# Mixing gates in eight tiles of the array, and a new order of the first 620 steps, in a fused convolution, feed-forward and LoRA kernel on one core

## The chip, the core and the metric

The kernel runs on one NeuronCore of a Trainium2 chip. A core has five engines that run side by side, each with its own stream of instructions: TensorE (PE, matrix products; PEld is its loading of the stationary operand), VectorE (DVE), ScalarE (ACT), GpSimd (POOL) and SyncE (SP, which here only issues transfers). Semaphores order them against each other. The metric is the device time of one execution in microseconds (us), as a median of runs; lower is better.

## What is computed

The input x has shape (64, 64, 1024). A grouped 1-D convolution (4 groups, 9 taps) with a conditioning term runs over it; its result, 4096 rows of 1024, goes through a 1024x1024 layer with a shared LoRA and a LoRA that is mixed by gates for each of 8 batches; and x is added at the end.

```python
out = lax.conv_general_dilated(x, weight, ..., padding=[(4, 4)], feature_group_count=4)
out = out + einsum('nd,od->no', c, c_weight)[:, :, None] + bias[None, :, None]
...
base_out = matmul(x, kernel) + bias
A_eff = einsum('bn,nri->bri', gate, lora_A)      # 16 adapters, rank 32, mixed for each of 8 batches
B_eff = einsum('bn,nor->bor', gate, lora_B)
Ax    = einsum('bri,bti->btr', A_eff, x)
delta = einsum('bor,btr->bto', B_eff, Ax)
delta = delta + einsum('or,btr->bto', lora_B_shared, einsum('ri,bti->btr', lora_A_shared, x))
...
return x + base_out + delta
```

The change touches how A_eff and B_eff are made.

## The kernel before

The 64 samples are worked in 16 pairs of tiles ("pairs" 0 to 15), and each pair in four groups g. Two pairs share one batch, so one set of mixed LoRA matrices serves two pairs.

**Precision.** Each operand of the large products is split into a high part and a low part (`hi_of`, `lo_of`), and each product is three matmuls: high by high, high by low, low by high. The splits are most of the work of ACT (the high part), DVE and POOL (the low part: a step ends in `v` for DVE or `p` for POOL).

**One pair.** `xload` fetches the input; the convolution is `xhi`, `xlo`, `conv` for pairs 0 to 2, and for later pairs a form with fewer products (`xdiff`, `xohi`, `xolo`, `xdhi`, `xdlo`, `convo`, `convd`, with `evmid` taking the middle product out of PSUM). `evac` adds the conditioning term, and `turned` transposes on DVE. The dense layer of pair 0 is 8 `plain` steps for each of four blocks (3 matmuls each). From pair 1 on it is 7 products of half-size blocks (`prod`, 12 matmuls each) in place of 8, with sums of blocks made ahead (`asum`, `wsum`) and behind (`xsum`, `ysum`, `radd`, `yadd`). `lora` multiplies by A_eff, and `delta` by B_eff and the bias. `total` adds the input row, and `store` writes. The shared LoRA is folded into the weights once: `fmm` makes a product, `fadd` adds it to the weight tile on DVE.

**The gates.** 16 adapters times 8 rows of a block are laid on the 128 partitions. `lload(w, i)` fetches a piece of lora_A (w=0) or lora_B (w=1), eight pieces each. `gmask` builds a matrix of 128 x 64 that holds the gates on a block diagonal: 8 blocks of 16 adapters. `mix(w, j)`, four for each w, does two matmuls: the stationary operand is that matrix, 128 x 64, the moving operand one piece, 128 x 512. The two write the lower and the upper 64 partitions of one PSUM tile. `mixout` copies that tile to SBUF on ACT, `mixput` writes it to a DRAM buffer `eff[w]` in two transfers, and `aload` and `bload` fetch from there what a batch needs.

**Order.** The text `ORDER` (line 50 on) lists all steps, one after another. Each engine runs its share of them strictly in that order, each queue of transfers too; a semaphore wait holds up everything behind it on the same engine. PSUM is divided by the pools into eight tiles of 128 x 512: two for convolutions (`pcv`), five for all 512-wide sums (`pmm`, tag `mm`: blocks of the dense layer, `fmm`, `mix`), one for `lora`.

Lines that the prediction's steps touch: 318 (`conv`), 364 (`evmid` on ACT), 376 (`evac`), 475 and 479 (`fmm`, `fadd`), 485 (`wsum`), 512 and 513 (`gmask`), 520 (`lload`), 528 (`mix`), 534 (`mixout`), 542 (`mixput`), 550 (`aload`), 556 (`bload`), 580 (`plain`), 592 (`prod`), 602 (`lora`).

Of the kernel before, what the change touches and what calls it, by code (L numbers as in the profile page):

```python
# [10 lines left out]
ALU = mybir.AluOpType  # L11
# [39 lines left out]
small 1, warm, twload 1, busy 29, twload 0, cwload, gload, ctload, cwide, cmul, thi 2, small 0, thi 0, tlo 0 v,  # L51
xload 0 0, xhi 0 0, tlo 2 p, xload 0 1, xlo 0 0 v, conv 0 0, twsum v, xhi 0 1, xlo 0 1 v, conv 0 1, sbload 1,
sbhi 1, csum, evac 0 0 v, turned 0 0, xload 0 2, xhi 0 2, xload 0 3, saload 0, sblo 1 p, xlo 0 2 p, evac 0 1 v,
turned 0 1, saload 1, gmask, xhi 0 3, conv 0 2, xlo 0 3 p, sahi 1, conv 0 3, sahi 0, salo 0 v, fmm 0 1,
sbload 0, sbhi 0, fmm 1 1, wload 1 0, evac 0 2 a, xload 1 0, sblo 0 v, fmm 1 0, salo 1 v, xload 1 1, xhi 1 0,
xhi 1 1, xlo 1 1 p, xlo 1 0 v, turned 0 2, yhi 0 0, ylo 0 0 p, wload 0 1, fadd 0 1, evac 0 3 a, fadd 1 0,
conv 1 0, whi 7 0, fmm 4 0, turned 0 3, xload 1 2, xhi 1 2, wlo 7 0 v, fmm 3 0, wload 1 1, conv 1 1, fadd 1 1,
wload 4 0, fmm 0 0, whi 0 1, wload 0 0, fadd 0 0, evac 1 0 a, plain 0 1 0, fadd 4 0, xlo 1 2 p, turned 1 0,
whi 0 0, wlo 0 1 p, fmm 2 1, fmm 2 0, yhi 0 7, evac 1 1 a, conv 1 2, fmm 5 0, wload 2 1, wload 2 0, fadd 2 0,
wlo 0 0 p, plain 0 0 0, xload 1 3, fadd 2 1, wload 5 0, xhi 1 3, fmm 4 1, xlo 1 3 p, plain 0 0 1, whi 0 2,  # L60
ylo 0 7 v, fadd 5 0, plain 0 3 0, whi 7 1, yhi 0 4, wload 3 0, fadd 3 0, whi 0 3, wload 5 1, fmm 3 1, conv 1 3,
turned 1 1, wlo 7 1 v, wload 3 1, xload 2 0, plain 0 1 1, fadd 3 1, whi 7 2, evac 1 2 v, wlo 7 2 p, wload 4 1,
wlo 0 3 p, wlo 0 2 v, lload 0 6, plain 0 2 0, whi 7 3, plain 0 3 1, fadd 4 1, wload 7 1, turned 1 2, whi 1 1,
plain 0 1 2, lload 0 7, xhi 2 0, plain 0 0 2, ylo 0 4 v, plain 0 3 2, xlo 2 0 v, plain 0 2 1, fmm 5 1,
evac 1 3 a, xload 3 0, wlo 7 3 v, plain 0 2 2, turned 1 3, whi 1 0, yhi 0 1, ylo 0 1 v, fadd 5 1, whi 6 1,
conv 2 0, wload 7 0, thi 1, xdiff 3 0 0 v, wload 6 0, evac 2 0 a, lload 1 5, wlo 1 0 p, fmm 7 0, fadd 7 0,
plain 0 2 3, plain 0 0 3, fmm 6 0, lload 0 2, plain 0 3 3, plain 0 1 3, fadd 6 0, lload 0 5, whi 6 0, asum 1 2,
yhi 1 2, lload 0 0, yhi 1 0, plain 0 0 4, plain 0 2 4, wsum 2 2 v, whi 2 2, lload 1 1, wlo 1 1 p, plain 0 0 5,
fmm 6 1, tlo 1 v, plain 0 2 5, rload 0 2, wlo 6 0 v, wsum 2 1 v, wsum 2 3 v, whi 1 2, wlo 1 2 v, plain 0 1 4,
whi 2 1, asum 1 3, whi 1 3, wlo 1 3 p, xload 2 2, wload 6 1, fadd 6 1, xload 2 1, whi 6 2, lload 0 1, xhi 2 2,  # L70
plain 0 3 4, lload 0 4, plain 0 2 6, lload 1 0, lload 0 3, wsum 2 0 v, fmm 7 1, plain 0 2 7, xload 2 3,
plain 0 0 6, fadd 7 1, whi 6 3, total 0 2, lload 1 6, mix 0 0, mixout 0 0 a, wlo 6 2 v, xhi 2 1, wlo 6 3 v,
wlo 6 1 v, wsum 3 2 v, xlo 2 2 v, mix 0 3, mixout 0 3 a, mix 0 2, mixout 0 2 a, wsum 3 0 v, wsum 5 0 v,
mixput 0 0, whi 2 3, mix 0 1, wsum 3 1 v, mix 1 0, mixput 0 3, mixout 0 1 a, xdiff 3 0 1 p, wsum 4 0 v,
conv 2 2, wlo 2 2 v, whi 2 0, wlo 2 0 v, ylo 1 2 v, plain 0 1 5, wsum 5 1 v, rload 0 0, wsum 5 2 v, wsum 4 2 v,
xlo 2 1 v, plain 0 0 7, mixput 0 1, ylo 1 0 p, mixput 0 2, wlo 2 1 v, prod 1 0, plain 0 1 6, wsum 3 3 v,
wsum 5 3 v, rload 0 1, plain 0 3 5, wsum 4 3 v, bihi, whi 3 2, keep 1 0, plain 0 1 7, lload 1 3, wsum 4 1 v,
plain 0 3 6, mixout 1 0 a, lload 1 7, mix 1 3, aload 0, whi 5 3, yhi 1 3, rload 0 3, lload 1 2, ylo 1 3 v,
mixout 1 3 a, total 0 1, lora 0, mix 1 1, turned 2 0, lora 1, whi 5 0, bilo, xohi 3 0, lload 1 4, mix 1 2,
whi 4 2, wlo 4 2 v, mixout 1 1 a, xolo 3 0 v, whi 3 0, wlo 3 0 v, wlo 3 2 v, yhi 1 1, ylo 1 1 v, mixout 1 2 a,  # L80
asum 1 5, total 0 0, whi 4 1, conv 2 1, axlow 1, axsum 1, xload 3 2, wlo 4 1 p, wlo 2 3 v, whi 4 0,
plain 0 3 7, axlow 0, axsum 0, mixput 1 0, mixput 1 3, wlo 4 0 v, xhi 2 3, xlo 2 3 v, wlo 5 3 v, axhi 1,
prod 1 1, biput 0, axlo 1, whi 3 3, asum 1 6, yhi 1 6, wlo 3 3 v, mixput 1 1, evac 2 1 a, turned 2 1, aload 1,
mixput 1 2, total 0 3, evac 2 2 v, turned 2 2, bload 0 0, whi 3 1, axhi 0, prod 1 2, keep 1 2, conv 2 3,
bhi 0 0, biput 1, yhi 2 0, evac 2 3 a, blo 0 0 v, axlo 0, yhi 1 4, bload 0 1, wlo 3 1 p, prod 1 3, ylo 2 0 v,
delta 0 0 1, total 0 0 1, bhi 0 1, blo 0 1 v, ylo 1 6 p, prod 1 6, whi 4 3, delta 0 3 1, wlo 4 3 v, store 0 0,
ylo 1 4 p, turned 2 3, delta 0 2 1, total 0 3 1, xdhi 3 0, convo 3 0, yhi 1 5, whi 5 1, ylo 1 5 v, xdlo 3 0 v,
delta 1 0, total 0 2 1, xload 3 1, keep 1 3, prod 1 4, evmid 3 0 a, store 0 3, xohi 3 1, xdiff 3 1 0 v,
xdiff 3 1 1 p, wlo 5 1 p, delta 0 1 1, total 0 1 1, wlo 5 0 v, xolo 3 1 p, convd 3 0, evac 3 0, turned 3 0,
asum 2 3, rload 1 0, convo 3 1, yhi 2 1, xdhi 3 1, xdlo 3 1 v, prod 2 0, whi 5 2, store 0 2, delta 1 2,  # L90
xload 3 3, keep 2 0, wlo 5 2 p, yhi 2 3, prod 1 5, total 1 0, xohi 3 3, xolo 3 3 v, asum 2 2, xdiff 3 2 0 p,
store 1 0, convo 3 3, evmid 3 1 a, xdiff 3 2 1 p, convd 3 1, ylo 2 3 v, prod 2 3, rload 1 3, delta 1 1,
ylo 2 1 v, xsum 1, asum 2 5, prod 2 1, xdhi 3 2, evac 3 1, turned 3 1, rload 1 2, radd 1 2 v, xdlo 3 2 v,
xdiff 3 3 0 v, delta 1 3, xohi 3 2, xdiff 3 3 1 p, yhi 2 5, xolo 3 2 v, ylo 2 5 p, yhi 2 2, ylo 2 2 v,
evmid 3 3 a, radd 1 3 v, convo 3 2, total 1 2, store 0 1, evmid 3 2 a, convd 3 2, xdhi 3 3, xdlo 3 3 v,
rload 1 1, radd 1 1 v, bload 1 0, lora 2, axlow 2, asum 2 6, prod 2 2, total 1 1, convd 3 3, evac 3 2,
turned 3 2, axsum 2, xload 4 0, xohi 4 0, xolo 4 0 p, bhi 1 0, yhi 2 4, ylo 2 4 v, axhi 2, prod 2 5, keep 2 3,
yhi 3 0, ysum 1 p, xdiff 4 0 0 v, xdiff 4 0 1 v, prod 2 4, store 1 1, xload 4 1, xohi 4 1, xolo 4 1 p,
yadd 1 v, blo 1 0 v, xdhi 4 0, axlo 2, delta 2 0, yhi 2 6, evac 3 3, keep 2 2, xdlo 4 0 v, convo 4 0,
turned 3 3, convd 4 0, rload 2 0, evmid 4 0 a, total 1 3, total 2 0, ylo 3 0 v, lora 3, xdiff 4 1 0 v,  # L100
xdiff 4 1 1 p, asum 3 3, yhi 3 3, prod 3 0, convo 4 1, ylo 3 3 v, evac 4 0, turned 4 0, xdhi 4 1, xload 4 3,
xohi 4 3, xdlo 4 1 v, asum 3 2, xolo 4 3 v, yhi 3 2, ylo 2 6 v, xload 4 2, xdiff 4 2 0 p, store 1 2,
xdiff 4 2 1 p, xohi 4 2, prod 3 3, yhi 3 1, bload 1 1, evmid 4 1 a, delta 2 2, ylo 3 2 v, xolo 4 2 v, asum 3 5,
store 2 0, convd 4 1, xdhi 4 2, xsum 2, convo 4 2, evmid 4 2 a, evac 4 1, xdlo 4 2 v, rload 2 2, radd 2 2 p,
total 2 2, xdiff 4 3 0 v, xdiff 4 3 1 p, prod 2 6, turned 4 1, yhi 3 4, bhi 1 1, convd 4 2, evac 4 2, keep 3 0,
prod 3 2, ylo 3 1 v, rload 2 3, radd 2 3 v, ysum 2 v, convo 4 3, yadd 2 v, xdhi 4 3, xdlo 4 3 v, ylo 3 4 v,
aload 2, prod 3 1, convd 4 3, turned 4 2, blo 1 1 p, xload 5 0, yhi 3 5, xohi 5 0, keep 3 2, asum 3 6,
keep 3 3, xload 5 1, xohi 5 1, delta 2 3, prod 3 4, delta 2 1, xdiff 5 0 0 p, xdiff 5 0 1 v, axlow 3,
ylo 3 5 p, evmid 4 3 a, total 2 3, prod 3 5, store 2 3, xolo 5 0 p, rload 2 1, yhi 3 6, radd 2 1 p, rload 3 0,
axsum 3, evac 4 3, axhi 3, turned 4 3, yhi 4 0, axlo 3, delta 3 0, xload 5 2, xdhi 5 0, store 1 3, xdlo 5 0 v,  # L110
# [707 lines left out]
```

## Time and profile before

| | |
|---|---|
| median of 3 runs | 447.79 us (447.44 to 451.44) |
| the profiled execution | 447.48 us, of which the span from the first to the last instruction is 445.7 us |
| granted TensorE clock over the span | 1.00 |
| bytes moved | 67.05 MB, mean 150 GB/s |
| mix matmuls (L528) | 32 records, first at 44.1 us, last at 63.3 us |
| lora matmuls (L602) | 512 records, from 59.4 to 420.4 us; the fifth `lora` step starts at 141.04 us |
| transfers of line 520, 256 KB each | 16, 4.6 us from issue to landing in the median |

A matmul of 32-bit operands leaves two records each: 16 mix products are 32 records. The 512-wide matmuls of the dense layer are shown at 391 ns each in a group row, but follow each other every 227 ns: they are pipelined, and it is the distance from start to start that costs time. On DVE a 128x512 instruction is shown at about 0.68 us and the next one starts 0.60 us after it.

### The profile page before, as it was taken

The page shows a single profiled execution, that of the slowest core. Times are in us where ns is not written, and L with a number is a line of the kernel's source. Part 1 is how long each engine was busy: PE and PEld are TensorE (multiplying, and loading weights), DVE is VectorE, ACT ScalarE, POOL GpSimd, SP SyncE. Part 2 cuts the span into 40 slices and gives each one's busy share as a digit, 9 for nine tenths or more (in the row PEclk, how much of TensorE's full clock was granted, in tenths as well). Part 3 has the DMA queues.
Part 4 walks back from the last instruction along what each step waited for, and adds up shares of the span by engine and source line. Part 5 has one row for each costly group of instructions (what it writes and reads, how often), then busy time and mean ns, then how long its engine had stood idle before and what let it go on. Part 6 is the DMA issues. An engine that isn't in the chain of part 4 may idle for free.

```text
span 445.7 us, 7717 instructions
## 1 busy us (share of the span) xinstructions
PE 438.3 (98%) x2557; PEld 358.7 (80%) x2557; DVE 391.3 (88%) x615; ACT 251.2 (56%) x639; POOL 234.5 (53%) x202
## 2 busy tenths in 40 slices
PE   8999999999999999999999999999999999999996
PEld 7677658888888888888878888888888888888884
DVE  5998979899899899889899899899798989887783
ACT  5877468556655566446555655646554745654440
POOL 3766024754747653555444445464656475467543
PEclk9999999999999999999999999999999999999999
DMA  8999582461625463534345453443536354262243
GB/s 229 300 280 308 147 251 66 142 186 49 186 82 158 136 190 110 170 120 136 97 139 147 151 182 91 119 142 90 175 98 186 95 169 151 72 222 90 91 150 118
DMA packets 52488, 67.05 MB, mean 150 GB/s; under 512 B 6112, under 2 KB 34016, under 8 KB 52448
## 3 DMA queue, kind: packets, MB, share of 16 engines
q1 hardware_dynamic: 42512, 49.83, 38.9%
q10 hardware_dynamic: 9936, 16.73, 10.2%
q8 instruction: 20, 0.33, 0.3%
q14 instruction: 20, 0.16, 0.1%
HBM read 47.65 MB, written 18.87 MB: 149 GB/s over the span
## 4 chain that ended last, share of the span: by engine, by line
PE 91%; DMA 4%; DVE 2%; issue 1%; SPq 0%; ACT 0%; ACTq 0%; DVEq 0%
PE mm_a L592 19%; PE mm_d L592 18%; PE mm_c L592 17%; PE mm_b L592 9%; PE cv L346 8%; PE cm L346 4%; PE axp L602 3%; PE cv L318 2%; DMA wr<-in_dram 2%; PE mx L528 2%; PE mm_a L580 1%; PE mm_c L580 1%; DMA ls<-in_dram 1%; DMA ctt<-in_dram 1%; PE mm_d L580 1%; PE mm_a L660 1%
## 5 line engine op out<-in xcount | busy, mean ns | idle before, releaser
L592 PE MATMUL mm_a<-wh,y 128*128 128x512 f32 x240 | 79.6, 392 | 0.0
L592 PE MATMUL mm_d<-wh,y 128*128 128x512 f32 x240 | 79.2, 391 | 0.0
L592 PE MATMUL mm_c<-wh,y 128*128 128x512 f32 x240 | 79.1, 391 | 0.0
L364 ACT ACTIVATE md<-cm,cadd 128x64 f32<-128x64 f32 x208 | 48.2, 315 | 44.8 <-PE cm L346 41.1
L326 POOL TENSOR_TENSOR xf<-xt 128x256 f32<-128x256 f32 x45 | 33.3, 747 | 49.4 <-DVE xd L270 39.4
L265 ACT CAST xd<-xf 128x512 fp32r<-128x512 f32 x52 | 32.5, 626 | 44.9 <-PE cv L346 20.7
L265 ACT CAST y<-s 128x512 fp32r<-128x512 f32 x60 | 37.2, 624 | 30.5 <-POOL s L412 15.3
L592 PEld LDWEIGHTS mm_a<-wh,y 128*128 128x128 f32 x240 | 45.1, 188 | 9.9 <-issue 0.4
L592 PEld LDWEIGHTS mm_d<-wh,y 128*128 128x128 f32 x240 | 45.1, 188 | 9.2 <-issue 0.2
L592 PEld LDWEIGHTS mm_c<-wh,y 128*128 128x128 f32 x240 | 45.1, 188 | 9.1 <-ACT c L636 0.2
L387 DVE STREAM_TRANSPOSE z<-v 128x512 f32<-128x512 f32 x64 | 45.4, 709 | 3.2 <-PE axp L602 1.9
L592 PE MATMUL mm_a<-wl,y 128*128 128x512 f32 x120 | 46.9, 391 | 0.0
L592 PE MATMUL mm_c<-wl,y 128*128 128x512 f32 x120 | 46.8, 390 | 0.0
L592 PE MATMUL mm_d<-wl,y 128*128 128x512 f32 x120 | 46.8, 390 | 0.0
L346 PE MATMUL cv<-xd,th 128*128 128x256 f32 x208 | 45.7, 282 | 0.4 <-DVE xd L270 0.4
L378 DVE TENSOR_TENSOR v<-cv,md 128x512 f32<-128x512 f32 x52 | 35.7, 686 | 7.7 <-PE cv L346 2.5
L270 DVE TENSOR_TENSOR xd<-xf,xd 128x512 fp32r<-128x512 f32 x41 | 34.5, 842 | 7.6 <-ACT xd L265 7.4
L270 DVE TENSOR_TENSOR y<-s,y 128x512 fp32r<-128x512 f32 x49 | 38.2, 782 | 3.0 <-ACT y L265 2.7
L592 PE MATMUL mm_b<-wh,y 128*128 128x512 f32 x120 | 39.6, 391 | 0.0
L346 PEld LDWEIGHTS cv<-xd,th 128*128 128x128 f32 x208 | 35.5, 188 | 2.4 <-DVE xd L270 0.6
L265 ACT CAST y<-z 128x512 fp32r<-128x512 f32 x49 | 30.6, 625 | 11.8 <-DVE c L641 4.5
L326 DVE TENSOR_TENSOR xf<-xt 128x256 f32<-128x256 f32 x59 | 33.7, 587 | 0.2
(132 smaller groups left out, 1008.2 us busy)
## 6 DMA issues: line engine op xcount, KB each, us to landing
xt<-in_dram SPq DMA_DIRECT2D x64, 258.0 KB, 3.2
r<-in_dram SPq DMA_DIRECT2D x64, 256.0 KB, 3.5
out_dram<-r ACTq DMA_DIRECT2D x63, 256.0 KB, 2.6
ls<-in_dram SPq DMA_DIRECT2D x16, 256.0 KB, 4.6
br<-eff SPq DMA_DIRECT2D x48, 64.0 KB, 2.8
wr<-in_dram SPq DMA_DIRECT2D x16, 176.0 KB, 4.2
eff<-ls SPq DMA_DIRECT2D x16, 128.0 KB, 2.7
wr<-in_dram SPq DMA_DIRECT2D x16, 80.0 KB, 3.9
```

The costliest lines, as they stand in the source:

```text
L265: nc.scalar.copy(dst, src)
L270: engs[eng].tensor_tensor(dst, src, f32(hi), ALU.subtract)
L318: nc.tensor.matmul(ps, a[:, 2 * kt, g, :], b[:, :, kt:kt + P], start=(n == 0), stop=(n == 5))
L326: engs[eng].tensor_tensor(xdf[p, g][:, e], m, odd(p, g), ALU.subtract)
L346: nc.tensor.matmul(ps, a[:, w, g, :], b, start=(n == 0), stop=(n == 2))
L364: nc.scalar.activation(t[:, n], cpm[p, g][:, n], ACTF.Identity, bias=c[:, n:n + 1])
L378: nc.vector.tensor_tensor(v.rearrange("p n (i e) -> p e n i", e=2), cps.pop((p, g)), mid.pop((p, g)).unsqueeze(1).to_broadcast([P, 2, 4, H ...
L387: nc.vector.transpose(z[:, :, :, :, gg, :], vs.pop((p, g)).rearrange("p m j -> p (m j)"))
L528: nc.tensor.matmul(mps[w, j][n * e:n * e + n], gm.rearrange("p b i -> p (b i)"), lraw[w, 2 * j + e], start=True, stop=True)
L580: nc.tensor.matmul(acc[p, BLOCKS[b]], m[:, kk, :], n, start=(k == 0 and q == 0), stop=(k == 7 and q == 2))
L592: nc.tensor.matmul(ps, a[:, k, :], b[bb, k], start=s, stop=(k == HK - 1 and q == 2), skip_group_check=not first)
L602: nc.tensor.matmul(axp[q * R:q * R + R, p % 2, :], a[:, k, :], zs[p, hf][:, k, :], start=k < 2, stop=k >= 6)
```

## The change

Two things are changed together.

First, the gates. The stationary matrix is cut in two by partitions: partitions 0 to 63 hold adapters times rows 0 to 3, partitions 64 to 127 rows 4 to 7. Each half is now 64 x 32 instead of being a half of a 128 x 64 matrix with zeros in it. A `mix(w, j)` takes four pieces and does eight matmuls, 64 x 32 stationary and 64 x 512 moving, into two PSUM tiles: four column places times two row halves. There are two `mix` steps for each w instead of four, `mixout` and `mixput` have one more argument, and the layout of `eff` follows. As many copies (8) and transfers (16 of 128 KB for `mixput`) as before.

Second, `ORDER`: the first 624 steps are replaced by 620 others in a new order. From the step `lora 4` on the list is the same, word for word, 1224 steps.

```diff
-    eff = [dram.tile([NC, NB * GC, AW], F32, ...) for w in range(2)]
+    HI = GC // 2
+    eff = [dram.tile([4, NB, 2, 2, 2, HI, AW], F32, ...) for w in range(2)]
-    gm = const.tile([P, NB, GC], F32, name="gm")
+    gm = const.tile([P, NB, HI], F32, name="gm")
...
-        nc.vector.tensor_reduce(mask, ident.rearrange("p (i n) -> p i n", i=GC), AX.X, ALU.add)
+        nc.vector.tensor_reduce(mask, ident.rearrange("p (r i n) -> p i r n", r=2, i=HI), AX.XY, ALU.add)
...
-        mps[w, j] = pl.tile([P, 2 * AW], F32, tag=tag, name=f"mx{w}_{j}")
-        n = NB * GC
-        for e in range(2):
-            nc.tensor.matmul(mps[w, j][n * e:n * e + n], gm.rearrange("p b i -> p (b i)"), lraw[w, 2 * j + e],
-                             start=True, stop=True)
+        for r in range(2):
+            mps[w, j, r] = pl.tile([P, 2 * AW], F32, tag=tag, name=f"mx{w}_{j}_{r}")
+        n, m = NB * HI, P // 2
+        for e in range(4):
+            for r in range(2):
+                nc.tensor.matmul(mps[w, j, r][n * e:n * e + n], gm[m * r:m * r + m].rearrange("p b i -> p (b i)"),
+                                 lraw[w, 2 * e + j][m * r:m * r + m], start=True, stop=True)
...
-    def mixput(w, j):
-        n = NB * GC
-        for e in range(2):
-            dst = eff[w].rearrange("c p a -> p c a")[:, 4 * j + 2 * e:4 * j + 2 * e + 2, :]
-            nc.sync.dma_start(dst, mev[w, j][n * e:n * e + n].rearrange("p (c a) -> p c a", c=2))
+    def mixput(w, j, r):
+        for c in range(2):
+            dst = eff[w][:, :, j, c, r].rearrange("e b i a -> (e b) i a")
+            nc.sync.dma_start(dst, mev[w, j, r][:, c * AW:c * AW + AW])
...
-        nc.sync.dma_start(ar[b].rearrange("p k r -> p (k r)"), eff[0][:, GC * b:GC * b + GC, :])
+        nc.sync.dma_start(ar[b].rearrange("p k r -> p (k r)"), eff[0][:, b].rearrange("e j c r i a -> e (j c r i a)"))
...
-        src = eff[1][:, GC * b:GC * b + GC, :].rearrange("c (e q) a -> c e (q a)", e=2)[:, :, HN * h:HN * h + HN]
+        src = eff[1][:, b].rearrange("e j c r i a -> e (j c r) (i a)")[:, :, HN * h:HN * h + HN]
```

The beginning of the old order and of the new one, and the stretches of the new one around the mixes:

```diff
-small 1, warm, twload 1, busy 29, twload 0, cwload, gload, ctload, cwide, cmul, thi 2, small 0, thi 0, tlo 0 v,
-xload 0 0, xhi 0 0, tlo 2 p, xload 0 1, xlo 0 0 v, conv 0 0, twsum v, xhi 0 1, xlo 0 1 v, conv 0 1, sbload 1,
-sbhi 1, csum, evac 0 0 v, turned 0 0, xload 0 2, xhi 0 2, xload 0 3, saload 0, sblo 1 p, xlo 0 2 p, evac 0 1 v,
-turned 0 1, saload 1, gmask, xhi 0 3, conv 0 2, xlo 0 3 p, sahi 1, conv 0 3, sahi 0, salo 0 v, fmm 0 1,
+saload 0, warm, busy 29, cwload, cwide, small 0, ctload, cmul, sahi 0, twload 1, xload 0 0, twload 0, small 1,
+xload 0 1, thi 2, salo 0 v, gload, thi 0, twsum v, tlo 0 v, xhi 0 0, xhi 0 1, xlo 0 0 v, tlo 2 p, conv 0 0,
+sbload 1, sbhi 1, sbload 0, wload 0 0, xload 0 2, xlo 0 1 v, sblo 1 v, fmm 3 1, xload 0 3, fmm 0 1, fmm 1 1,
+sbhi 0, gmask, sblo 0 v, fmm 0 0, csum, xhi 0 2, fadd 0 0, whi 0 0, evac 0 0 v, turned 0 0, conv 0 1,
+evac 0 1 v, bihi, wload 0 1, fadd 0 1, wload 1 0, turned 0 1, xlo 0 2 p, xhi 0 3, fmm 2 0, wlo 0 0 p, conv 0 2,
+xload 1 0, xhi 1 0, wload 2 0, wsum 2 0 v, xlo 0 3 p, conv 0 3, yhi 0 0, xlo 1 0 v, saload 1, whi 7 0,
+evac 0 2 v, wlo 7 0 p, turned 0 2, sahi 1, salo 1 v, thi 1, xload 1 1, xhi 1 1, xlo 1 1 p, fmm 1 0, conv 1 0,
...
+whi 3 0, wsum 5 1 p, plain 0 3 1, plain 0 2 7, rload 0 0, total 0 2, wsum 2 2 v, plain 0 0 5, plain 0 1 4,
+mix 0 1, plain 0 0 6, xlo 2 0 v, whi 6 3, plain 0 3 2, lload 1 0, mixout 0 1 0 a, lload 0 6, mixout 0 1 1 a,
+mix 0 0, wlo 6 3 v, lload 1 6, mixout 0 0 0 a, xload 2 1, whi 2 2, plain 0 3 3, plain 0 0 7, xhi 2 1,
...
+prod 1 0, plain 0 3 4, lload 1 4, asum 1 3, mixput 0 0 0, mixput 0 1 0, mixput 0 1 1, wsum 3 3 v, whi 2 3,
+wlo 2 2 v, wsum 4 1 v, xlo 2 1 v, wlo 2 0 v, whi 6 2, wlo 6 2 v, mixout 0 0 1 a, mixput 0 0 1, total 0 0,
+yhi 1 3, wsum 5 3 v, mix 1 0, plain 0 3 5, mixout 1 0 0 a, xload 2 2, plain 0 1 6, conv 2 1, wsum 5 2 v, bilo,
+lload 1 7, lload 1 5, wsum 4 2 v, whi 3 1, wsum 4 3 v, wlo 2 3 p, plain 0 1 7, evac 2 0 a, wlo 3 1 v, xhi 2 2,
+wlo 3 2 v, mixout 1 0 1 a, whi 2 1, asum 1 2, wsum 4 0 v, whi 5 3, plain 0 3 6, xload 3 0, wlo 3 0 v, mix 1 1,
+aload 0, lora 0, ylo 1 3 v, whi 3 3, xlo 2 2 v, xdiff 3 0 0 v, xdiff 3 0 1 v, mixout 1 1 0 a, mixout 1 1 1 a,
```

In the replaced stretch some steps also go to another engine. Net, DVE has 197 instructions there instead of 192, ACT 199 instead of 219 (five `evmid` steps of pairs 3 to 5 go from ACT, four instructions each, to DVE, one each), POOL 67 as before, SP 123 as before, PE 674 instead of 658. Everything else that is computed is the same.

## The prediction

> **What bounds the kernel now.** I read the page first: busy time by engine, and the chain that ended last.
>
> ```profile
> PE 438.3 (98%) x2557; PEld 358.7 (80%) x2557; DVE 391.3 (88%) x615; ACT 251.2 (56%) x639; POOL 234.5 (53%) x202
> ...
> PE 91%; DMA 4%; DVE 2%; issue 1%; SPq 0%; ACT 0%; ACTq 0%; DVEq 0%
> ```
>
> TensorE is the bound, VectorE is next to it. A busy PE need not be a full one, so I checked the distances: 45 matmuls start from 25 to 35 us, one per 0.222 us, against 0.227 us between 512-wide matmuls of the dense layer. So PE has no holes there, and what is to shorten the span must take work from PE, or remove holes at the start. The second view is busy time in stretches (columns: stretch, its length, then busy us and instructions of PE, PEld, DVE, ACT, POOL, then clock, DMA share, GB/s). 138.6 us is where DVE starts the first instruction of the part of the list that is not changed.
>
> ```profile
> 0.00:12.00 12.00, 10.17 (x53) 8.96 (x54) 7.20 (x11) 5.65 (x9) 4.75 (x10) 1.00 0.85 229
> 12.00:138.60 126.60, 125.51 (x680) 96.66 (x679) 116.33 (x180) 81.82 (x198) 67.15 (x56) 1.00 0.61 182
> 138.60:214.00 75.40, 75.40 (x460) 63.21 (x459) 67.94 (x110) 43.69 (x113) 41.74 (x36) 1.00 0.47 141
> 214.00:234.00 20.00, 19.57 (x127) 16.16 (x126) 18.98 (x30) 11.41 (x34) 8.15 (x9) 1.00 0.37 117
> ```
>
> DVE is busy for 92% of the changed stretch after 12 us, 90% up to 214 us and 95% up to 234 us, where PE has to wait for it once (0.43 us). ACT and POOL have room. The third view is the timeline of PE around the mixes: the rows tell from start to start what a mix costs.
>
> ```profile
> 44.10 4.74 PE L528 MATMUL mx<-ls,gm 128*64 128x512 f32 x20
> 48.77 0.50 PE L318 MATMUL cv<-xsh,th 128*128 128x512 f32 x1
> ...
> 57.19 2.24 PE L528 MATMUL mx<-ls,gm 128*64 128x512 f32 x4
> 59.36 1.08 PE L602 MATMUL axp<-z,ar 128*32 128x128 f32 x32
> 60.80 1.08 PE L528 MATMUL mx<-ls,gm 128*64 128x512 f32 x4 [0.35 <-DMA ls<-in_dram]
> 61.81 1.08 PE L602 MATMUL axp<-z,ar 128*32 128x128 f32 x32
> 62.82 1.08 PE L528 MATMUL mx<-ls,gm 128*64 128x512 f32 x4
> 63.83 0.50 PE L318 MATMUL cv<-xs,th 128*128 128x512 f32 x1
> ```
>
> The last view is the first microseconds of PE, DVE and ACT, where transfers and splits set the pace.
>
> ```profile
> 7.47 0.48 PE L318 MATMUL cv<-xsh,th 128*128 128x512 f32 x1
> 11.62 0.51 PE L318 MATMUL cv<-xsl,th 128*128 128x512 f32 x1 [0.62 <-POOL xsl L270]
> 16.35 0.50 PE L318 MATMUL cv<-xsl,th 128*128 128x512 f32 x1 [0.37 <-DVE xsl L270]
> 4.78 1.50 DVE L727 COPY cwe<-cwt 128x512 f32<-128x512 f32 x1 [3.65 <-DMA cwt<-in_dram]
> 12.43 0.99 DVE L513 TENSOR_TENSOR gm<-gg,mask 128x64 f32<-128x64 f32 x1
> 8.15 0.62 ACT L265 CAST sb<-sbr 96x512 fp32r<-96x512 f32 x1 [1.23 <-DMA sbr<-in_dram]
> ```
>
> **The mixes.** Removed: eight mixes of two products, four records each. From start to start: 4.67 us for five (44.10 to 48.77), 2.17 for one (57.19 to 59.36, with waits for a piece and for `aload 0`), 1.01 for each of the last two, and 0.35 us of waiting ahead of one: 9.2 us, of which about 1.6 are waits. Added: four mixes of eight products. Inside a mix of before the two products run side by side: its four records start in two pairs, 0.43 us apart, so a mix is two rounds of 0.43 us and 0.15 us for entering and leaving, 1.01 us alone. `lora` does the same with four products of 32 columns: its 32 records start in eight groups of four, 0.11 us apart. If all eight tiles of a new mix run at once, it is again two rounds, 1.01 us, and some 7 ns for each further start: 1.07 us, 4.3 us for four. What no row of this trace shows is two row halves at once. The ends: at once, 4.3 us; in turn, four rounds, 1.87 us each, 7.5 us. The Trainium skill, "TensorE: Matmul & The Clock Gate", section "Part 3: Packing small matmuls", measured 6.32 times for nine tiles and 10.6 for sixteen, so about 5.6 for eight (an estimate from its table): eight products alone, 8 x 0.86 = 6.8 us, by 5.6 are 1.22 us, with 0.15 for entering 1.37 us, 5.5 us for four. The rows of the trace give two and four columns at nearly their full factor, so I take their side: 4.3 us, a gain of 9.2 - 4.3 = 4.9 us with the waits gone. By the skill's figure it is 3.7 us, in turn 1.7 us.
>
> A rule that speaks against the change: the Trainium skill, "TensorEngine Tiling (Array Packing)", section "Gotcha 1: PSUM Pressure", says that row tiles write to different PSUM banks, and so need more of them. Here a mix takes two of the five tiles `mm` at once. Three blocks of pair 0 hold the other three, so `mix 0 0` must wait for both copies of `mix 0 1`. In the list two `plain` steps (6 matmuls, 1.36 us) stand between; two copies of 0.59 us (line 534) need 1.2 us. Hidden, just; without that cover up to 1.2 us. I charge nothing.
>
> **The start.** Here the new list does more ahead of the first convolutions. By the trace, DVE instructions follow each other at 0.60 us, and transfers land at the pace of before (bytes in order of issue). `saload 0` (192 KB) and `xload 0 0` now stand ahead of `twload 0`, so both halves of the convolution's weights are in at about 7.2 us, not before 4.6 us. Then on DVE: `twsum`, `tlo 0`, `xlo 0 0` end at 9.0 us; the third matmul of the first convolution starts at about 9.1 us and the sixth ends its turn at 10.0 us (before: 8.95). Behind it stand four `fmm`, ahead of the second convolution. The first waits for `sblo 1` (10.2 us). The fourth waits for `sblo 0`, which stands on DVE behind mask and gates (0.3 + 0.8, the 0.99 row with half the columns): 12 us. The second convolution, queued behind it, starts at 12.2 us; before it started at 8.96. From there `conv 0 2` follows at 13.9, `conv 0 3` waits for POOL (`xlo 0 3` behind `wlo 0 0`, 1.3 us each) to 16.6, `conv 1 0` for `evac 0 2` on DVE, which frees its PSUM tile at 18.0, `conv 1 1` for `evac 0 3` on ACT (20.0), `conv 1 2` for `evac 1 0` (22.2). The first `plain` step ends at 24.4 us. Work done by then: 42 matmuls of line 318 at 0.236, 9 of line 475 at 0.235, 3 of line 580 at 0.227, together 12.7 us: 11.7 us behind the clock. Before, at 25 us: 42, 10 and 11 matmuls, 14.8 us: 10.3 behind. So 1.4 us are lost at the start, 1.5 taken; the ends are 0 (transfers land earlier) and 3 us. From 24 us on I find the splits ahead of the `plain` steps by 0.5 us and more.
>
> **VectorE.** DVE gets five instructions more (0.69 us, line 376 or 378, 0.60 from start to start), and with the other exchanges about 2.6 us. Before, it was busy for 123.5 of 138.6 us; the 15 us of idle time are 4.5 at the start, about 5 released by PE, about 3 by ACT. Now: 123.5 + 2.6 = 126.1 busy, 5.3 at the start, 3 to 5 by ACT: 134.4 to 136.4 us. PE, 3.4 us earlier (4.9 - 1.5), wants it at 135.2 us. So the gain can just pass, at 97% busy from 12 us on; I charge 0.6 us. If the cover is gone, see the second rival. Past `lora 4` nothing is changed; DVE has 7.5 idle us up to 214 us, more than half of it released by PE, which shrink when PE is early.
>
> **Queues.** ACT loses 20 instructions (5 x 0.93 us), nothing is late for it. POOL: same count. SP: same transfers in another order; the two pieces `lload 1 7` and `lload 1 5` stand behind `mixput 0 0 1`, which waits for `mixout 0 0 1` on ACT, and `mix 1 1` needs them. I find that copy near 50 us, the pieces landing (4.2 us and two issues) near 56 us and PE there at 57: hidden, by a microsecond; before, such waits were the 1.6 us at 57 to 61 us. They could come back as 0 to 2 us; I charge 0.4. `aload`, `bload`, `biput`, `store`: same sizes and counts, covered as before by what PE does meanwhile.
>
> **Sum**, on the profiled execution of 447.48 us: -4.9 + 1.5 + 0.6 + 0.4 = -2.4, 445.1 us. The median stands 0.31 above that execution, so 445.4 us.
>
> **Rivals.**
> First, all of it lands: no loss at the start, no wait on DVE: 447.8 - 4.9 = 442.9, and 442.4 if the wait of 0.43 us at 233 us goes too. For it: PE's holes of before at the start (0.62 and 0.37 us) show that waits there are short. Against it: the walk above.
> Second, slower: VectorE becomes the bound of the changed stretch. If it stays only as dense as before, 92% after 12 us, its 126.1 - 7.2 = 118.9 us need 129.4 us, with 0.8 us more at the start 142.2 us in place of 138.6: 3.6 us later, 451.4 us; the unchanged part can give some back from its idle time. It decides from 94.5% on: above that the change gains. For it: 95% from 214 to 234 us is the densest such stretch of the unchanged part, and only with PE waiting. Against: about a third of its idle time was PE's doing.
> Third, the rows take their turn, or PE's gain is eaten by waits for pieces: -1.7 + 1.5 + 0.6 + 0.4 = +0.8, 448.6 us.
>
> **How the numbers follow.** A measurement of this kernel can tell about 1%, 4.5 us. The forecast (443.5 to 447) 0.47, all lands 0.15 (nearly all of it over 1%), third rival (447 to 449.5) 0.16, slower (449.5 to 454 and beyond) 0.22, of which 0.15 are over 1%. Faster by over 1% (below 443.3): 0.14; within: 0.71. The range for 8 in 10 reaches from 442.4 to 451.8; the forecast's own is 443.5 to 447.
>
> **What would show it.** Four mixes of 16 records in about 1.07 us each (eight starts within 0.1 us, then again after 0.43 us): the gain; 1.9 us: rows in turn. The second convolution starting near 12 us, and the first `plain` step near 24 us. `lora 4` on PE near 138 us in place of 141.04. DVE's busy share from 12 us on 95% or more, and DVE among the releasers of PE between 70 and 234 us. It would be wrong if PE shows several waits for DVE, or for `ls`, of over a microsecond after 40 us.

## The result, and the profile after

The changed kernel takes 453.3 us in the median of nine runs (451.3 to 455.4), the kernel before 447.8 us: a ratio of 1.010 (95% interval 1.007 to 1.013). It is slower by 1%, and outside the range of the prediction. The profiled execution took 453.34 us, its span is 451.6 us. Two slow executions among the experiments, one of 615 us (`after_w512_again`, the profiled one, so that it has no distances below) and one of 2,470 us (`before_y160`), are left out of all figures.

The page's first and fourth part of the changed kernel:

```profile
PE 441.2 (98%) x2589; PEld 357.2 (79%) x2589; DVE 394.4 (87%) x620; ACT 246.5 (55%) x619; POOL 236.6 (52%) x202
...
PE 79%; DMA 8%; DVE 7%; issue 3%; SPq 2%; ACT 1%; POOL 1%; DVEq 0%; ACTq 0%; POOLq 0%
```

TensorE was to save 4.9 us on the mixes and their waits, and is busy 2.9 us longer than before. Busy time by stretches (columns as in the prediction: stretch, length, PE, PEld, DVE, ACT, POOL, clock, DMA share, GB/s):

```profile
0.00:12.00 12.00, 9.48 (x46) 8.14 (x46) 5.39 (x11) 5.68 (x9) 2.24 (x8) 1.00 0.79 216
12.00:138.60 126.60, 123.66 (x715) 95.56 (x715) 116.17 (x185) 76.26 (x177) 70.45 (x56) 1.00 0.59 183
138.60:214.00 75.40, 75.27 (x453) 61.86 (x452) 68.66 (x108) 43.23 (x112) 41.52 (x35) 1.00 0.44 137
214.00:234.00 20.00, 20.00 (x129) 16.59 (x128) 17.41 (x28) 10.90 (x31) 9.29 (x9) 1.00 0.37 118
```

From 138.6 to 234 us, where (but for the first 3 us) the list of steps is the same word for word, PE is idle for 0.13 of 95.4 us, at full clock, and yet does 582 matmuls where it did 587 before. DVE is busy for 91% and 87% of the two stretches (before 90% and 95%). So no engine holds PE up there: PE itself does its work more slowly. (The chain in the fourth part leaves PE more often than before, 79% against 91%, but in this stretch without idle time of PE.) The mixes are not the reason; PE's timeline around them:

```profile
42.75 1.09 PE L532 MATMUL mx<-ls,gm 64*32 64x512 f32 x16
...
45.37 1.09 PE L532 MATMUL mx<-ls,gm 64*32 64x512 f32 x16
...
53.59 1.09 PE L532 MATMUL mx<-ls,gm 64*32 64x512 f32 x16
...
59.01 1.42 PE L532 MATMUL mx<-ls,gm 64*32 64x512 f32 x16
62.02 1.19 PE L605 MATMUL axp<-z,ar 128*32 128x128 f32 x36 [1.59 <-DMA ar<-eff]
```

Three mixes take 1.02 us from start to start, the fourth 0.33 longer, and then the first `lora` waits 1.59 us for its piece of A_eff. The cost is in the dense layer. The group rows of its products (busy us in all, mean ns of one), first of the kernel before, then of the changed one:

```profile
L592 PE MATMUL mm_a<-wh,y 128*128 128x512 f32 x240 | 79.6, 392 | 0.0
L592 PE MATMUL mm_d<-wh,y 128*128 128x512 f32 x240 | 79.2, 391 | 0.0
```

```profile
L595 PE MATMUL mm_a<-wh,y 128*128 128x512 f32 x240 | 80.6, 396 | 0.0
L595 PE MATMUL mm_d<-wh,y 128*128 128x512 f32 x240 | 80.4, 396 | 0.0
```

Each is about 5 ns longer, with no idle time ahead of it. The timeline shows the same from start to start, before and after, near 301 us:

```profile
301.12 0.40 PE L592 MATMUL mm_d<-wh,y 128*128 128x512 f32 x1
301.35 0.39 PE L592 MATMUL mm_d<-wl,y 128*128 128x512 f32 x1
301.58 0.62 PE L592 MATMUL mm_d<-wh,y 128*128 128x512 f32 x2
302.03 0.39 PE L592 MATMUL mm_d<-wl,y 128*128 128x512 f32 x1
302.26 0.62 PE L592 MATMUL mm_d<-wh,y 128*128 128x512 f32 x2
```

```profile
300.12 0.62 PE L595 MATMUL mm_c<-wh,y 128*128 128x512 f32 x2
300.58 0.40 PE L595 MATMUL mm_c<-wl,y 128*128 128x512 f32 x1
300.82 0.62 PE L595 MATMUL mm_c<-wh,y 128*128 128x512 f32 x2
301.28 0.40 PE L595 MATMUL mm_c<-wl,y 128*128 128x512 f32 x1
301.52 0.62 PE L595 MATMUL mm_c<-wh,y 128*128 128x512 f32 x2
```

Before, five starts take 1.14 us, 228 ns each; after, six take 1.40 us, 233 ns. Over the whole trace the mean is 228.4 ns before and 233.5 ns after (distances within one line of the dense layer, those over 260 ns left out). There are 1,356 such products, and as many records: their operands are cast to fp32r (line 265), and each leaves one record; it is the products of plain float32, the mixes and `lora`, that leave two. 1,356 x 5.1 ns = 6.9 us. The other matmuls keep their distances (the half-size convolution 117 to 118 ns, line 318 at 236 ns in both), so it is not the clock. A span 5.9 us longer is thus 6.9 us lost in the dense products and about 1 us gained elsewhere.

### The profile page after: what moved, and what is told of

It is laid out like the page before. It is cut to its first block, busy times and chain, and to the rows that moved or that the text cites. A ratio compares the mean times of both kernels' runs of the same rounds, so it can differ in the third digit from the quotient of the medians.

```text
span 451.6 us, 7752 instructions
## 1 busy us (share of the span) xinstructions
PE 441.2 (98%) x2589; PEld 357.2 (79%) x2589; DVE 394.4 (87%) x620; ACT 246.5 (55%) x619; POOL 236.6 (52%) x202
## 4 chain that ended last, share of the span: by engine, by line
PE 79%; DMA 8%; DVE 7%; issue 3%; SPq 2%; ACT 1%; POOL 1%; DVEq 0%; ACTq 0%; POOLq 0%
PE mm_a L595 16%; PE mm_d L595 15%; PE mm_c L595 15%; PE mm_b L595 8%; PE cv L346 7%; PE cm L346 4%; PE axp L605 3%; DMA xt<-in_dram 2%; PE cv L318 2%; DMA ar<-eff 1%; DMA gg<-in_dram 1%; PE mm_a L583 1%; PE mm_c L583 1%; DMA r<-in_dram 1%; DMA out_dram<-r 1%
## 5 line engine op out<-in xcount | busy, mean ns | idle before, releaser
L595 PE MATMUL mm_a<-wh,y 128*128 128x512 f32 x240 | 80.6, 396 | 0.0
L595 PE MATMUL mm_d<-wh,y 128*128 128x512 f32 x240 | 80.4, 396 | 0.0
L595 PE MATMUL mm_c<-wh,y 128*128 128x512 f32 x240 | 80.4, 396 | 0.0
L364 ACT ACTIVATE md<-cm,cadd 128x64 f32<-128x64 f32 x188 | 43.7, 316 | 37.5 <-PE cm L346 33.3
L270 DVE TENSOR_TENSOR y<-s,y 128x512 fp32r<-128x512 f32 x48 | 37.1, 775 | 4.4 <-ACT y L265 4.1
L270 DVE TENSOR_TENSOR xd<-xf,xd 128x512 fp32r<-128x512 f32 x41 | 32.7, 798 | 4.7 <-ACT xd L265 4.3
L270 POOL TENSOR_TENSOR xd<-xf,xd 128x512 fp32r<-128x512 f32 x11 | 15.2, 1384 | 34.1 <-ACT xd L265 34.1
```

The source lines that it names most:

```text
L270: engs[eng].tensor_tensor(dst, src, f32(hi), ALU.subtract)
L364: nc.scalar.activation(t[:, n], cpm[p, g][:, n], ACTF.Identity, bias=c[:, n:n + 1])
L595: nc.tensor.matmul(ps, a[:, k, :], b[bb, k], start=s, stop=(k == HK - 1 and q == 2), skip_group_check=not first)
```

## The experiments

**What could make one kind of product slower.** Where the tiles lie in SBUF is read from the compiled kernels. A pool gives its tags their places in the order of first use, so a new order of steps moves them. The dense products read a weight tile (moving operand, tag `w`: `wh`, `wl`) and a tile `y` (stationary). Their start addresses modulo 512 are 320 and 320 in the kernel before, 32 and 192 in the changed one. My first theory was that a weight tile that starts 32 past a multiple of 64 is read more slowly; the rival, that the pace comes with the new order in some other way. Four kernels, each with small unused tiles put ahead of others:

```diff
 after_w64:   -saload 0, warm, busy 29, ...
              +pad 8 gapa, saload 0, warm, pad 8 gapb, busy 29, ...      (two tiles of 8 floats around tag w)
 before_w32:  -conv 0 1, sbload 1, sbhi 1, ...
              +conv 0 1, pad 8 gapa, sbload 1, pad 8 gapb, sbhi 1, ...
 after_all64: +    const.tile([P, 8], F32, name="gap")
              and the slots of xsh, xsl, xs rounded up to a multiple of 64 bytes
 after_w512:  after_all64 with  +pad 112 gapa, saload 0, ...
+    def pad(n, name):
+        work.tile([P, n], F32, tag=name, name=name, bufs=1)
```

> The changed kernel, with 32 bytes of unused SBUF before the tiles of the weights (the moving operand of all dense products) and 32 after them: the weight tiles start at a multiple of 64 bytes again, as in the kernel before, and by pads nothing else changes its place by other than 64 bytes. Theory (place of the weight tiles): the dense products' distance from start to start falls from 232 ns to 227 ns, 1,350 of them by 5 ns are 6.7 us, and the time falls from 453.3 to about 446.6 us. Rival (the chip or the run was slower, or the mixes leave TensorE slower): 232 ns stays, about 453 us. Rival (VectorE is the bound): 232 ns or less, and the time stays within 1.5 us of 453.

> The kernel before, with 32 unused bytes before the weight tiles and 32 after them, so that they start 32 bytes past a multiple of 64. Nothing else is changed. Theory (place of the weight tiles): the distance rises from 227 to 232 ns, and the time from 447.8 to about 454 us. Rivals: 227 ns and 447.8 us stay.

> The changed kernel with every operand of TensorE but the inputs of the first three pairs' convolutions at a multiple of 64 bytes (a pad behind the gates, and longer slots for the split inputs). If the place of any moving operand counts, the 256-wide convolution products (118 ns, 468 of them) and the 64 products with the bias row (236 ns) get faster as well, by 2 to 9 ns each: 1.5 to 3 us below the run that moves the weight tiles alone, some 444 us. If only the weight tiles count: as that run. If places don't count: 453 us.

> As the run before, with the weight tiles at a multiple of 512 bytes instead of 64. If a coarser grid than 64 bytes counts, the distance falls below 227 ns, down to 213 ns at the least (two rounds of the mix took 0.427 us for 512 columns), that is up to 19 us less. If 64 bytes is the grid, 227 ns and the same time as the run before within 1 us.

In kind, all four went as the first theory said: 228.6 to 229.8 ns for the three with `w` at a multiple of 64, 233.0 ns and a ratio of 1.011 for the kernel before with `w` moved by 32. (All numbers are in the table below.) In time, `after_w64` came down to 449.2 us only, where 446.6 was written, and neither the further gain of other operands (some 444 us) nor that of a coarser grid came. The loss is the place of the tiles, then, not the order's waits. Two more kernels go with them: `before_all64`, the kernel before with the same rounding of the slots,

> The kernel before with every operand of TensorE but the inputs of the first three convolutions at a multiple of 64 bytes; its weight tiles were there already. If the weight tiles are nearly all of the effect: 447.8 us within 1 us. If the other operands count too: up to 2 us less, and the ranking of the two kernels at equal places changes by as much.

which changed nothing in time (1.0004), so rounding by itself brings no gain; and `after_w512` once more, on another chip,

> The kernel with the weight tiles at multiples of 512 bytes once more, as the base of the three others on this chip. If its first result was no accident of a chip, its ratio to the kernel before is 0.997 again (0.995 to 0.999), with a mean of 228.6 ns from start to start of the dense products.

which gave 0.998 (0.996 to 0.999).

**The first theory falls.** Here only `y` is moved, in `after_w512`, with the weight tiles left at multiples of 512 (the tags behind `y` move by 64 bytes in the first, by 256 in the second):

```diff
 w512_y32:  -xload 1 0, ...
            +pad 8 gapy, xload 1 0, pad 8 gapz, ...      (xload 1 0 makes the first tile of tag y)
 w512_y64:  +pad 16 gapy, xload 1 0, pad 48 gapz, ...
```

> The base, with the other operand of the dense products (the stationary one, the tiles `y`) moved by 32 bytes, from 256 to 288 in 512; the weight tiles stay at multiples of 512. Theory (the place of the moving operand alone counts): mean distance of the dense products 228.5 to 230 ns, time as the base within 2 us. Rival (either operand at 32 past a multiple of 64 costs 5 ns): 233 ns, and 6 to 7 us more than the base.

> The base, with the stationary operand `y` moved by 64 bytes, from 256 to 320 in 512, the weight tiles as in the base. If the small second effect is one of the distance between the two operands (a difference of 64 in 256 costs, none at a multiple of 256): the difference is now 192 in 256, so the mean distance is over 229.3 ns if any non-zero difference counts, and 228.6 ns if only 64 does or if the effect has another cause. Time within 2 us of the base either way.

Both lost the gain, at 232.9 and 233.2 ns. The first alone could be read as "either operand at 32 past a multiple of 64"; the second, with both operands at multiples of 64, cannot, and it lost 3.6 us against its base where I had written within 2. The difference of the two places, modulo 256, which I had taken for a small second effect, fits all runs so far. As it was seen only behind these results, four more kernels tested it: the changed kernel with only `y` moved, so that the difference is 0 again while the weight tiles stay at 32 past a multiple of 64; the kernel before with the difference of the changed one; and two differences not seen until then.

```diff
 after_y96:    +pad 24 gapy, xload 1 0, pad 40 gapz, ...
 before_y160:  +pad 40 gapy, xload 1 0, pad 24 gapz, ...
 w512_y128:    +pad 32 gapy, xload 1 0, pad 32 gapz, ...
 w512_y224:    +pad 56 gapy, xload 1 0, pad 8 gapz, ...
```

> The changed kernel, with one thing moved: the tiles `y` (stationary operand of the dense products) by 96 bytes, from 192 to 288 in 512. The weight tiles, the moving operand, stay at 32 past a multiple of 64; the difference of the two is then a multiple of 256 as in the kernel before. Theory (the pace follows the difference of the two operands' places, modulo 256): mean distance of the dense products 228.3 to 229 ns in place of 233.5, span 446 to 448 us, time 447 to 449 us. Rival (a moving operand at 32 past a multiple of 64 costs 5 ns each): it stays at 233 ns, and at 453 us.

> The kernel before, with the tiles `y` moved by 160 bytes, from 320 to 480 in 512; the weight tiles stay at a multiple of 64 (320 in 512). The difference is then what it is in the changed kernel (96 in 256). Theory of the difference: 233.5 ns in the mean in place of 228.4, some 6.5 us longer: 454 to 455.5 us. Rival (place of the moving operand alone): as the kernel before.

> The version with weight tiles at multiples of 512, with `y` moved by 128 bytes, to 384 in 512: a difference of 128 in 256, not seen so far. Theory of the difference: it lies on a curve with 228.6 ns at 0, 229.8 at 64, 233.5 at 96, 233.2 at 192 and 232.9 at 224; I expect 231 to 235 ns, and 450 to 454 us. Rival (place of the moving operand alone): 228.6 ns, and 447.7 us.

> The same with `y` moved by 224 bytes, to 480 in 512: a difference of 32 in 256, not seen so far. Theory of the difference: between 228.6 and 233.5 ns, over 229.3; 448.5 to 454 us. Rival (place of the moving operand alone): 228.6 ns, and 447.7 us.

Each time is a ratio to the kernel before, measured beside it; each distance is the mean of one profiled execution, and `w512_y224` was run twice only.

| kernel | w, y (mod 512) | w - y (mod 256) | mean ns, start to start | time against the kernel before (95%) |
|---|---|---|---|---|
| before | 320, 320 | 0 | 228.4 | 1 |
| before_all64 | 448, 448 | 0 | 228.8 | 1.000 (0.999 to 1.002) |
| after_all64 | 64, 320 | 0 | 228.9 | 0.999 (0.998 to 1.001) |
| after_w512 | 0, 256 | 0 | 228.6 | 0.997 (0.995 to 0.999) |
| after_y96 | 32, 288 | 0 | 228.5 | 0.996 (0.995 to 0.998) |
| w512_y224 | 0, 480 | 32 | 233.2 | 1.007 (1.004 to 1.010) |
| after_w64 | 64, 256 | 64 | 229.8 | 1.001 (0.999 to 1.003) |
| after | 32, 192 | 96 | 233.5 | 1.010 (1.007 to 1.013) |
| before_y160 | 320, 480 | 96 | 233.6 | 1.010 (1.007 to 1.013) |
| w512_y128 | 0, 384 | 128 | 232.7 | 1.007 (1.006 to 1.009) |
| w512_y64 | 0, 320 | 192 | 233.2 | 1.006 (1.005 to 1.008) |
| w512_y32 | 0, 288 | 224 | 232.9 | 1.007 (1.004 to 1.009) |
| before_w32 | 352, 384 | 224 | 233.0 | 1.011 (1.007 to 1.015) |

Kernels with one difference agree whatever their order and their absolute places: 96 in two orders (233.5, 233.6), 224 in two (232.9, 233.0), 0 in five places. A difference of 0 in 512 (before) and one of 256 in 512 (`after_w512`) are alike, so it is 256 that counts. No place of one operand alone does it: `w` at 0 and `y` at 320 stand in quick rows, and together in a slow one. The group rows of `after_y96`, and then of `before_y160`, have changed sides against the rows above:

```profile
L596 PE MATMUL mm_a<-wh,y 128*128 128x512 f32 x240 | 79.4, 392 | 0.0
L596 PE MATMUL mm_d<-wh,y 128*128 128x512 f32 x240 | 79.1, 391 | 0.0
```

```profile
L592 PE MATMUL mm_a<-wh,y 128*128 128x512 f32 x240 | 80.8, 397 | 0.0
L592 PE MATMUL mm_d<-wh,y 128*128 128x512 f32 x240 | 80.5, 396 | 0.0
```

So 96 bytes ahead of the tag `y` take the loss out of the changed kernel (a ratio of 0.996 in place of 1.010) and bring its own gain to light, and 160 bytes put the same loss into the kernel before (454.7 against 448.9 us on that chip). The smaller gate tile lies ahead of both tags and moves both by the same 128 bytes, so it is the order of first use that changed the difference. Why the difference of two addresses sets the pace was not tried.

**The gates without the new order.** The old order, with the four new mixes in the places of old ones, and the tiles where they lie in the kernel before:

```diff
-mix 0 0, ... mix 0 3, ... mix 0 2, ... mix 0 1, ... mix 1 0, ... mix 1 3, ... mix 1 1, ... mix 1 2
+mix 0 0, ...              mix 0 1, ...                            mix 1 1, ...              mix 1 0
```

> The old order of steps, with the four new mixes put where eight old ones stood, and the tiles where they are in the kernel before. If the mixes' TensorE time is what they are worth in place: the first group of five old mixes (4.7 us) becomes two new ones of 1.02 us with a wait of 1.2 us for the two copies between them, and the other three (4.5 us with waits) become two: 3 to 4 us less than before, 444.5 us. If what follows was waiting for something else anyway (the split of the next convolution's input on VectorE, the LoRA matrices from DRAM): less than 1.5 us, 446.5 to 448 us.

A miss: 452.5 us on a chip where the kernel before takes 449.0, a ratio of 1.008 (1.006 to 1.010), at a mean distance of 228.3 ns. The eight-tile mixes alone do not make the kernel faster. PE's list of waits (us in total, times, longest):

```profile
PE dl L664 <- DVE axt L627: 2.4, 1, 2.4
PE mx L533 <- DVE r L670: 1.2, 1, 1.2
...
PE mx L533 <- ACT ls L539: 0.7, 1, 0.7
```

The last line is the cost that the prediction named and charged nothing for: a mix takes two of the five `mm` tiles at once, and `mix 0 1` waits for the copy of a tile of `mix 0 0`. The old order has no two `plain` steps there to cover it. The second line is the same shortage once more: the second half of a mix waits until a `total` on DVE gives a tile back. The first line, a `delta` of pair 0 waiting for the LoRA sums, costs more than its 2.4 us. The stretches ahead of it, the wait, and behind it:

```profile
62.00:75.60 13.60, 13.11 (x70) 9.51 (x67) 12.11 (x19) 10.41 (x25) 5.74 (x4) 1.00 0.32 101
75.60:78.20 2.60, 0.41 (x2) 0.00 (x0) 1.98 (x4) 1.63 (x5) 0.00 (x0) 1.00 0.32 87
78.20:82.20 4.00, 3.75 (x10) 3.01 (x11) 3.20 (x6) 3.48 (x9) 1.28 (x1) 0.60 0.37 131
```

In the 4 us behind the wait the granted clock is 0.60 in the mean (0.50 from 79.0 to 82.4 us), and PE starts 10 matmuls where it starts 17 or 18 at full clock: 4.0 x 0.4 = 1.6 us more. The waits and the clock are 5.9 us (2.4 + 1.2 + 0.7 + 1.6), of which 1.2 stood in the expectation: 4.7 of the some 7 us between a gain of 3.3 and a loss of 3.5. The rest was not traced.

**The wait ahead of the first `lora`.** In the changed kernel `aload 0` is issued at 55.4 us and its data lands at 62. Two ways to take the 1.4 to 1.6 us back, both from `after_w512`, and one that also changes the start:

```diff
 after_ar:         -mix 1 1, aload 0, lora 0, ...
                   +... mixput 0 0 1, aload 0, ...  mix 1 1, lora 0, ...
 after_ar_start:   after_ar, with twload 1, twload 0, small 1, xload 0 0, xload 0 1 ahead of saload 0
 w512_conv_ahead:  -mix 1 1, aload 0, lora 0, ylo 1 3 v, whi 3 3, xlo 2 2 v, ... conv 2 2, ...
                   +mix 1 1, aload 0, ylo 1 3 v, whi 3 3, xlo 2 2 v, conv 2 2, lora 0, ...
```

> The changed kernel with the weight tiles at 512 bytes, and the load of the first mixed lora_A ahead of three other loads in SyncE's queue. In the changed kernel the first lora step waits 1.6 us for that load. Expected: the load is issued 2 to 3 us earlier and the wait goes, some 1.5 us less than the same kernel with the load where it was (447.7 us), 446.2 us; but if VectorE holds TensorE back soon after, the wait comes back as another one before 100 us and the time is within 0.5 us of 447.7.

A miss: 449.3 us, a ratio of 1.001 (1.000 to 1.002) where `after_w512` has 0.997. The wait went from `lora 0` to `mix 1 1`. In SP's queue (start, length of the issues) `aload 0` now stands ahead of the last two pieces:

```profile
46.32 6.28 SPq L548 DMA_DIRECT2D eff<-ls  x8
54.38 0.65 SPq L556 DMA_DIRECT2D ar<-eff  x1
55.09 0.42 SPq L293 DMA_DIRECT2D xt<-in_dram  x1
55.56 0.98 SPq L525 DMA_DIRECT2D ls<-in_dram  x2
```

In `after_w512` the pieces are issued at 52.5 us, here at 55.6, since the queue stands 1.8 us (52.60 to 54.38) at `aload 0`; `mix 1 1` waits 1.62 us (the list of waits puts it down to ACT, the queue to its pieces). And again the clock falls: the stretches of that wait and behind it,

```profile
57.00:60.60 3.60, 2.05 (x7) 0.69 (x5) 1.72 (x4) 1.08 (x3) 0.00 (x0) 1.00 1.03 301
60.60:64.60 4.00, 3.92 (x58) 2.32 (x62) 1.97 (x5) 3.68 (x9) 0.43 (x1) 0.57 0.98 334
```

> As the run before, and the start as it was in the kernel before in one respect: both halves of the convolution's weights are loaded first, then the inputs, then the shared LoRA. Expected: the first convolution starts near 7.6 us instead of 8.9, and 1 to 1.5 us of the 1.9 lost at the start come back: some 445 us. If VectorE is the bound of the stretch up to 140 us, it gives less than 0.5 us.

A miss too: 452.1 us, 1.008 (1.006 to 1.010). The first convolution starts 0.5 us earlier than in `after_w512` (7.17 us), but an `fmm` then waits 2.5 us for its operand, the clock is 0.56 for the 3.8 us behind, and the second convolution starts at 13.4 us in place of 11.6. The rearranged first uses have also moved the tiles, to a difference of 64: 229.9 ns.

> The base, with the steps `ylo 1 3 v`, `whi 3 3`, `xlo 2 2 v` and `conv 2 2` moved ahead of `lora 0`, so that TensorE has six convolution products to do while the piece of A_eff for `lora 0` is still on its way. Theory (the wait of 1.4 us ahead of `lora 0` is a hole on the path that sets the end, and its cover was taken away by the gain of the mixes): the wait goes, `lora 4` starts 1.2 to 1.4 us earlier than in the base, near 137.6 us, and the span is 1 to 1.4 us shorter, near 443.9 us; time near 446.4 us. Rival (VectorE is as dense as TensorE there and takes the gain back): the wait for the piece goes, but waits for VectorE appear behind it, and `lora 4` starts within 0.5 us of the base. A second rival: the later `lora 0` makes a wait at the first `delta` as in the old order with the new mixes.

The wait for the piece is gone, as intended, and nothing is gained: 448.05 us, 0.997 (0.995 to 0.999), beside 448.2 us of its base on the same chip, and `lora 4` at 138.99 us where the base, profiled on another chip, has 138.92. The list of waits of PE from 55 us on begins with:

```profile
PE cv L348 <- ACT v L376: 1.0, 1, 1.0
PE cv L348 <- DVE xd L270: 0.4, 1, 0.4
PE mm_c L598 <- DVE y L270: 0.4, 1, 0.4
PE cm L348 <- ACT md L366: 0.3, 1, 0.3
```

Its rival said this in kind: PE runs into the next late producer. The largest wait is for ACT, at 74.3 us, not for VectorE.

## Why the prediction was wrong

**The step that failed** is a term of the sum that was put at nothing: "Past `lora 4` nothing is changed". The sum took every dense product at the 227 ns of the kernel before and asked only what the change does to other work. The new order moves the tiles, since a pool places a tag at its first use, and each dense product then takes 5.1 ns longer. The term left out is +6.9 us; with it the sum is -2.4 + 6.9 = +4.5, 452.0 us for the profiled execution, which took 453.34.

**The mixes: right.** Forecast 1.07 us each, measured 1.02 where nothing is waited for: the eight tiles, two row halves among them, run at once. The estimate from the table of the Trainium skill, "TensorE: Matmul & The Clock Gate", "Part 3: Packing small matmuls" (1.37 us), and "rows in turn" (1.87 us) are out. The wait of `mix 0 0` for its PSUM tiles was hidden, as written: it starts 0.33 us behind the last `plain` matmul, like the first mix.

**The start: right within its ends.** The second convolution starts at 12.88 us (forecast 12.2); the first `plain` step starts at 24.88 and ends its turn at 25.58 (forecast 24.4 for the end). Summing what each PE start in the first 40 us is late against the usual distance of its shape gives 4.6 us, against 2.2 before: 2.4 us in place of 1.5. It scatters: over three variants of each order that share the first steps (before, `before_w32`, `before_y160`; after, `after_y96`, `after_w512`) it is 2.2 to 3.4 and 3.2 to 4.6 us, 1.4 between the means.

**Waits for pieces: too small.** Charged 0.4 us; measured 0.33 inside the last mix and 1.59 at `lora 0`, 1.9 us. (At `lora 0` it scatters: 0.3 to 1.9 us in the nine kernels with the new order.) The text looked at the pieces `ls` and set `aload` aside as "covered as before by what PE does meanwhile". But nothing is left for PE to do meanwhile: all mixes are done at 60.43 us, where the kernel before had two of them behind `lora 0`. SP's queue, the first line of the kernel before, then the changed one:

```profile
54.82 0.56 SPq L550 DMA_DIRECT2D ar<-eff  x1
```

```profile
47.23 5.79 SPq L545 DMA_DIRECT2D eff<-ls  x8
53.07 0.58 SPq L293 DMA_DIRECT2D xt<-in_dram  x1
53.75 0.95 SPq L522 DMA_DIRECT2D ls<-in_dram  x2
54.76 0.46 SPq L293 DMA_DIRECT2D xt<-in_dram  x1
55.39 0.66 SPq L553 DMA_DIRECT2D ar<-eff  x1
```

Before, `lora 0` starts at 59.36 us, 4.5 us behind the issue of `aload 0`. Here the load stands behind eight transfers and four loads, is issued 0.6 us later, and takes 6.6 us to land. Why it takes 2 us longer is open: the DMA engines are as full (a share of 1.00 from 55.4 to 62 us, 0.98 from 54.8 to 59.4 us before).

**`lora 4`: right at equal pace.** It starts at 141.81 us, forecast near 138. It has 360 of the dense products ahead of it, 1.8 us of the loss; without that, 140.0. Taken over all variants, each with its own pace put back to 228.4 ns (the excess of its mean distance times 360 ahead of `lora 4`, times 996 behind it, is subtracted), `lora 4` starts at 141.0 to 142.5 us in four kernels with the old order (old mixes) and at 137.6 to 140.0 in nine with the new order and the changes above to the tiles' places alone: a gain of 3.1 us between the means. The forecast was 3.0 (141.04 to 138; PE's timeline has 140.97 for the first), the sum 2.4.

**VectorE: charged 0.6 us, not seen.** PE waits for DVE for 0.9 us from 12 to 138.6 us, all of it before 20 us and so part of the start. At equal pace too DVE stays under the 95% that the text named as a sign: in `after_y96` it is busy for 116.1 of 124.6 us (12 to 136.6), 93%.

**Behind `lora 4`: a second miss, hidden by the first.** The text let the gain of the head pass to the end. With the pace put back in the same way, the rest takes 304.1 to 305.1 us in the four kernels with the old order and 304.7 to 305.0 in the five new ones with a slow pace, but 305.9 to 306.9 in the four with a pace of 228.5 to 229.8 ns. So the unchanged part gives back 1 to 2 us of the gain when PE is both early and quick. In part it shows among the waits of PE after 138 us; in `after_y96`:

```profile
PE cv L347 <- DVE xd L271: 0.4, 1, 0.4
PE cm L347 <- ACT md L365: 0.3, 1, 0.3
PE cv L347 <- DVE v L379: 0.3, 1, 0.3
PE mm_c L596 <- DVE y L271: 0.2, 1, 0.2
```

The kernel before has only the first of these, and so has `after_w512`, where the rest takes 305.9 us. The waits too short for this list were not traced further, so the cause of this miss stays open in the main.

**The rivals.** The second gave 451.4 us, near the result by luck, by a mechanism that did not happen: VectorE is busy for 91.8% of 12 to 138.6 us, and after 20 us PE does not wait for it. The third (448.6 us) is right in one half: waits for pieces do eat gain, but the rows do not take turns. The first (442.9 us) would have needed no waits at all; the best version run, `after_y96`, is at 0.996 (0.995 to 0.998) of the kernel before, 448.0 against 448.9 us on its chip. So with the tiles in place the change gains 0.9 of the 2.4 us of the sum.

## What to carry to other kernels

A new order of steps, or a tile of another size between two others, moves where tiles lie against each other: before a changed order is judged, compare the mean start-to-start distance of the commonest matmul in both traces, and put the two operands back to the same distance in SBUF if it differs. A forecast that moves first uses should carry this as a term, here 5 ns by 1,356 products. A wait that is taken away is worth only what the next late producer lets through, and a wait of a few microseconds on TensorE can cost 1.7 to 2 times its length where the clock falls behind it (three waits here), and its own length where it doesn't.

## What the runs showed of the hardware that was not expected

- The pace of a 512-column matmul of fp32r operands, stationary 128 x 128, depends on the difference of the operands' addresses in SBUF modulo 256 bytes: 228.3 to 228.9 ns at 0, 229.8 to 229.9 at 64, 232.7 to 233.6 at 32, 96, 128, 192 and 224 (160 was not run). The absolute places, multiples of 64 or not, make no difference beyond 0.6 ns.
- Eight tiles of 64 x 32 (four column places, two row halves) work at once on float32 operands: 1.02 us for eight products of 512 columns, as long as two of 128 x 64 before.
- Behind three waits on TensorE the granted clock was 0.50 for 3.4 us, beginning 0.2 to 0.5 us after the wait's end: 2.44 us (`old_order_new_mix`, 79.0 to 82.4 us), 2.48 us (`after_ar_start`, 11.7 to 15.1) and 1.62 us (`after_ar`, 61.2 to 64.6). After 1.59 us in the changed kernel and 1.90 us in `after_all64` it stayed at 1.00, so the length alone does not tell. The Trainium skill, "TensorE: Matmul & The Clock Gate", "Part 1: The HAM clock gate", has half the clock after an idle window of about 3.4 us that runs freely; the half clock and the 3.4 us agree, but here shorter idle times were enough. Free windows fit too: in the three traces the clock falls 21, 2 and 16 times 3.413 us after the first clock record. On that count the wait of the changed kernel is cut by the end of a window at 60.75 us; but that of `after_all64` is not, so this is not the whole rule.
